# A four-layer attention and expert kernel: depooled rows by index gather, keys moved to layer 2, the last expert pair inside layer 3, select masks, turned maxima

## The chip, the cores and the metric

The kernel runs on one core of one Trainium2 chip. Its time is the device time of one execution in microseconds (us); the median of several runs is given. The profile comes from one more execution with the hardware profiler on. The engines are called PE (TensorE matmul), PEld (TensorE weight load), DVE (VectorE), ACT (ScalarE), POOL (GpSimd) and SP (SyncE, which here issues most of the DMAs).

## The reference

The input `x` is 16 batches of 256 tokens of 256 numbers. It passes through four layers, each an attention followed by a feed-forward part. `ctx` is 16 x 256 x 512.

- Layer 0: layer norm, causal-length masked self-attention with 16 heads of 16 and a bias; then 8 experts (256 to 1024 to 256, gelu), top 2, each expert with a capacity.
- Layer 1: the "depool". From the patches of `ctx` a decayed scan over the 256 patch positions of a batch gives `depool`; for each token an index `plug` picks one of its rows. The core of it:

```python
_, s = jax.lax.associative_scan(comb, (a_b, u), axis=1)
depool = s.reshape(bsz, plen, D_MODEL)
plug = jnp.clip(jnp.cumsum(boundary_mask, axis=1) - 1, 0, plen - 1)
depool_out = depool[jnp.arange(bsz)[:, None], plug]
return depool_out + h
```

  with `h` the doubly normalised token times `W_in`. Then a feed-forward part with 8 routed experts (top 2) and a shared one.
- Layer 2: a cross-attention with 8 heads of 32 over keys and values from `ctx`, then causal self-attention with 16 heads of 16, then 4 unlike experts (2 chosen of 4).
- Layer 3: a cross-attention with 8 heads of 32 over keys and values from `ctx`, and a linear layer with fake fp8 quantisation, whose scale needs the maximum over all batches.

Softmax is taken with the true row maximum subtracted. All matmuls are float32 (two passes on PE each, as the records of the profile count them) except masks and selections, which are bfloat16.

## The kernel before

All of it is one program, in the order of the layers. Each stage is a loop over batches, or over experts. The activations `xs[b]` stay on chip as tiles of 128 x 2 x 256 (two halves t of 128 tokens). Where many batches overlap, the order of the instructions is written by hand: `order` is a pair of lists, one for even and one for odd steps s, of entries (function, lag, arguments). In step s each entry runs its function for batch s - lag (`do`, L432, skips batches outside 0 to 15). Inside `manual_schedule` the engines get their instructions exactly in this order, so every engine works through a queue of its own and waits for what is missing.

Stretches in time (us from the start of the span), with lines:

- **0 to 355, layer 0** (L536 to L760): attention with `heads_transposed` (L277: four 128x128 transposes into one PSUM tile, then an evacuation by ACT), `maxima` (L631), `exps`, `values`. Softmax subtracts the row maxima by an extra row of the head's padding: `maxima` (DVE, L635) writes minus the maximum into column 17 of the padded queries `qpads`; then `queries(..., QMs)` transposes those padded queries a second time, maximum included, so `QM` times `kpad` gives scores less maxima. `score_max` and `probs` (L223, L241) each take four PSUM banks of the pool `pmm` (six banks in layer 0 and layer 3, four in layer 2). Routing, and `scatter` (L730), which zeroes and fills the experts' buffers in DRAM.
- **355 to 410**: constants of layer 1, and keys and values of the first `KV0 = 3` batches for layers 2 and 3 (`kv_load`, `kv_piece`, L476 to L516: four pieces a batch of eight passes each).
- **410 to 882, layer-0 experts** (L889 to L928): 8 experts, weights by DMA, `pmm` and `pacc` matmuls of 512 and 256 columns. In between, DVE computes the patch ends and the plug indices (`mark`, `plugs`, L837 to L850); for batches 0 and 1 `patch_load`, `patch_norm` and `patch_scan` (L854 to L885) run here.
- **882 to 1118, depool** (L930 to L1040): `gather` (four indirect DMAs a batch on POOL, L945), `summed` (L951: adds the experts' rows, layer norm moments, a second norm by `rms_of_normed`, seven small POOL operations), `norm1`, `turned1`, `depool` (L976), `norm2`, `experts_in`, `gates`; and, for batches 2 to 15, `patch_load`, `patch_norm`, `patch_scan`; and `kv_bring`/`kv_part` for batches 3 to 15. The row `plug` is picked by a matmul: `patch_scan` transposes the plug column (L882), compares it with the partition number (L885) into a one-hot `take`, and `depool` multiplies `take` with `dep` (L984) in the same PSUM group as `W_in` (L982).
- **1118 to 1553**: router and shared expert, then 36 expert blocks of layer 1.
- **1553 to 2643, layer 2** (L1276 to L1812): one order for the cross-attention (class `Heads32`, L297), the self-attention, and the expert work of earlier batches. The experts work on pairs of batches: `f_in`, `f_turned`, `f_part`, `f_end` (L1659 to L1747) with lags 3 to 5. The steps start some 57 to 60 us apart; the first four hold no expert work, and after 2490 only expert work of the last pair is left. Causal masks are strips of bfloat16 matmuls into PSUM: `mask` before the maxima, `maskT` before the exps (both `strips`, L1471; the matmul is L1475). Weights come by `fetch` (L1639). Reciprocal square roots are two POOL operations (`rsqrt`, L154 to L158).
- **2643 to 2711, overflow** (L1815 to L1871): experts whose token count exceeds half of their region do the rest in blocks under `tc.If`, with all experts' weights loaded once beforehand (`FW`); sizes 128, 128, 256, 512, 512, 512. In this input expert 0 has 318 tokens past the half, expert 1 none, expert 2 30, expert 3 124.
- **2711 to 3010, layer 3** (L1880 to L2045): weights and constants, the first batches' loads, norms and queries, then the attention, order L2033 to L2045 (`fetch`, L1969, is an indirect DMA on POOL).
- **3010 to 3068**: maximum over all `zn`, and the fp8 linear layer.

Of the kernel before, what the change touches and what calls it, by code (L numbers as in the profile page):

```python
# [31 lines left out]
KV0 = 3  # L32

# [5 lines left out]
def tile_kernel(ctx: ExitStack, tc: tile.TileContext, a, out):  # L39
# [39 lines left out]
    selw = ct([P, 2, P], "selw")  # L79
    V.memset(selw, 0.0)  # L80
    for c in range(2):
        for j in range(4):
            for k in range(3):
                G.affine_select(
                    selw[:, c, :], selw[:, c, :], [[0, P]], ALU.not_equal, 1.0,
                    base=-(32 * j + 2 * k + c), channel_multiplier=1,
                )
    V.tensor_copy(sel, selw)
# [80 lines left out]
    def ln_stats(b, premul=1.0):  # L169
# [6 lines left out]
        r = small(2, "lnr")  # L176
# [9 lines left out]
    def rms_of_normed(mv, r, eps):  # L186


        q = small(2, "rmsq")
        G.tensor_tensor(q, r, r, ALU.mult)  # L190
        G.tensor_tensor(q, q, mv[:, :, 1], ALU.mult)
        rr = small(2, "rmsr")
        rsqrt(rr, q, 1.0, eps, 2)
        return rr
# [45 lines left out]

    def probs(cp, kc, QT, KT, n, bias, scale, minus=None, mask=None, causal=False):  # L241

        q0 = kc * P if causal else 0
        sc = [pmm().rearrange("p (i q) -> p i q", i=2)[:, :, q0:] for j in range(4)]
        if mask is not None:
            for j in range(4):
                mask(sc[j], j)
        for i in range(2):
# [5 lines left out]
            for j in range(4):  # L254
                rows = slice(32 * j, 32 * j + n)
                T.matmul(  # L256
                    sc[j][:, i, :], lhsT=KT[rows, c, kc * P : (kc + 1) * P], rhs=QT[rows, c, q0:],
                    start=(minus is None and mask is None), stop=True, skip_group_check=(mask is not None),
                )
# [17 lines left out]
    def heads_transposed(dst, src, h0, on=None, scale=None):  # L277
# [4 lines left out]
        evac(dst, p, scale, on=on)  # L282

# [160 lines left out]
    with ExitStack() as l01:  # L444
# [26 lines left out]
        b_key = col(a["b_src"][:D], 2, "b_key", c01)  # L471
        b_val = row_bc(a["b_src"][D:], D, "b_val", c01)
        mcol = t01([P, NT], "mcol")
# [58 lines left out]
        with ExitStack() as l0:  # L532
# [6 lines left out]
            bk = c0.tile([B, S], F32, name="bk")  # L539
# [22 lines left out]

            kpads, vpads = [], []
            for i in range(3):
                k = c0.tile([P, 4, S], F32, name=f"kpad{i}")
                V.memset(k, 1.0)
# [18 lines left out]
            def load(b):  # L585
# [17 lines left out]
                dma(ye2[n0 : n0 + 512, :].rearrange("(p r) d -> p (r d)", p=P), zero[:, : 4 * (D - 64)])  # L603
                if b == B - 1:
# [13 lines left out]
            def q_norm(b):  # L618
                mv, r = mvs.pop(b)
                qps[b] = qpads[2 * (b % 2) : 2 * (b % 2) + 2]  # L620
                for t in range(2):
                    normed(qps[b][t][:, :, :16], b, t, mv, r, split=16)
                    G.memset(qps[b][t][:, :, 17], 0.0)
# [4 lines left out]
            def queries(b, t, to):  # L628
                heads_transposed(to[b][:, :, t * P : (t + 1) * P], qps[b][t], 0, A)
# [1497 lines left out]
```

## Time and profile before

| | us |
|---|---|
| median of 3 runs | 3068.09 (3065.16 to 3077.72) |
| the profiled execution's own time | 3069.45 |
| its span in the trace | 3067.6 |
| mean granted clock of TensorE | 0.949 |

So 1.85 us of the profiled execution lie around the span. A page of the profile is read like this: first the busy time of each engine; then the span in 40 slices of 76.7 us; then DMA queues; then the chain of work that ended last; then groups of instructions by line, with mean duration in ns, and the idle time in front of them and what ended it. "PEclk" is the TensorE clock that the throttle granted, as a part of full speed.

Busy time by stage, from the same trace:

| stretch | length | PE | DVE | ACT | POOL | PEclk |
|---|---|---|---|---|---|---|
| 355 to 410, transition | 55 | 33.39 | 20.30 | 4.77 | 38.81 | 0.73 |
| 1118 to 1265, router, shared expert | 147 | 139.51 | 45.79 | 17.04 | 61.69 | 0.97 |
| 1265 to 1553, expert blocks | 288 | 286.18 | 66.02 | 53.55 | 9.86 | 1.00 |
| 3010 to 3068, fp8 linear | 58 | 24.55 | 42.22 | 21.33 | 24.39 | 0.55 |

A busy share is a mean over the stretch; a PE at 1.00 of its clock and near the whole stretch busy has no room, one at 0.57 with half of the time idle has.

### The profile page before, as it was taken

Reading aid. Unit: us, or ns where it says so; the run is one execution under the profiler, and the core shown is the slowest. Engines: PE = TensorE matmul, PEld = TensorE weight load, DVE = VectorE, ACT = ScalarE, POOL = GpSimd, SP = SyncE. Lnnn points to the kernel's source line nnn. Section 1 sums busy time; section 2 is a strip of 40 time slices with the busy share of each in tenths; the row PEclk is TensorE's granted clock in tenths of the full one; section 3 lists DMA queues with packets and bytes.
Section 4 is the critical chain, followed back from the end, with each engine's and each line's share of the span. In section 5 each row is a group of like instructions: output and inputs, shape, how many; then the busy total and the mean of one; then the engine's idle time right before and its main releaser. Section 6 shows DMA issues by size and latency. Waiting matters only on the chain. (4 is left out here: it accounts for less than half of the span.)

```text
span 3067.6 us, 57308 instructions
## 1 busy us (share of the span) xinstructions
PE 2807.7 (92%) x22567; PEld 2021.2 (66%) x22567; DVE 1475.1 (48%) x3848; ACT 1160.2 (38%) x2192; POOL 912.5 (30%) x1459
## 2 busy tenths in 40 slices
PE   7999799999989999999958789999999999759995
PEld 4666566666668865788834457777777777646663
DVE  7777611100027653222235666666666551038876
ACT  3555421121112221111113446566666664225453
POOL 2356620000036516200021333323333221045633
PEclk9999899999999999999967999999999999869996
DMA  6851232122135523666530113343333236342211
GB/s 251 343 194 57 74 109 85 56 69 78 40 101 180 161 90 126 222 198 200 183 120 18 34 55 102 103 128 107 102 120 99 90 98 208 97 136 64 67 35 55
DMA packets 249375, 357.07 MB, mean 116 GB/s; under 512 B 24107, under 2 KB 189019, under 8 KB 244868
## 3 DMA queue, kind: packets, MB, share of 16 engines
q1 hardware_dynamic: 230660, 305.75, 30.7%
q0 software_dynamic: 18432, 47.47, 4.8%
q8 instruction: 187, 3.06, 0.4%
q14 instruction: 96, 0.79, 0.1%
HBM read 236.40 MB, written 117.52 MB: 115 GB/s over the span
## 5 line engine op out<-in xcount | busy, mean ns | idle before, releaser
L263 ACT ACTIVATE big<-pmm 128x512 f32<-128x512 f32 (+1 forms) x512 | 237.0, 549 | 105.9 <-PE pmm L256 105.7
L909 PE MATMUL pmm<-xiT,w 128*128 128x512 f32 x512 | 225.3, 598 | 2.0 <-DVE xiT L145 2.0
L157 POOL TENSOR_SCALAR rsq<-mv 128x2 f32<-128x2 f32 x128 | 26.3, 206 | 666.8 <-DVE mv L175 652.1
L917 PE MATMUL pacc<-w,h 128*128 128x256 f32 x1024 | 223.6, 379 | 0.0
L918 DVE COPY yo<-pacc 128x256 f32<-128x256 f32 x64 | 27.2, 424 | 403.5 <-PE pacc L917 403.5
L917 PEld LDWEIGHTS pacc<-w,h 128*128 128x128 f32 x1024 | 194.6, 190 | 33.3 <-issue 7.7
L945 POOL DMA_INDIRECT y<-ye,idx x64 | 62.3, 974 | 481.5 <-issue 481.1
L635 DVE TENSOR_REDUCE qpad<-pmm 128x2 f32<-128x512 f32 x256 | 158.8, 684 | 55.0 <-PE pmm L234 54.4
L909 PEld LDWEIGHTS pmm<-xiT,w 128*128 128x128 f32 x512 | 96.1, 191 | 120.9 <-issue 111.8
L316 DVE TENSOR_REDUCE max<-pmm 128x2 f32<-128x512 f32 x256 | 158.4, 680 | 26.6 <-PE pmm L234 26.3
L1492 DVE TENSOR_REDUCE qpad<-pmm 128x2 f32<-128x256 f32 (+1 forms) x256 | 124.9, 551 | 70.0 <-PE pmm L234 70.0
L1676 PE MATMUL pf<-hf,fw 128*128 128x256 f32 x640 | 152.5, 381 | 0.0
L1376 POOL DMA_INDIRECT y<-yslots,idx x64 | 66.1, 1033 | 284.1 <-SPq L1259 267.9
L1676 PE MATMUL pf<-xf,fw 128*128 128x256 f32 x576 | 142.7, 384 | 0.1
L911 ACT ACTIVATE h<-pmm 128x512 f32<-128x512 f32 x128 | 76.4, 597 | 150.8 <-PE pmm L909 150.8
L1676 PEld LDWEIGHTS pf<-hf,fw 128*128 128x128 f32 x640 | 116.8, 190 | 15.6 <-issue 2.0
L272 PE MATMUL pacc<-big,vpad 128*32 128x256 f32 (+1 forms) x2048 | 121.2, 360 | 0.1
L1676 PEld LDWEIGHTS pf<-xf,fw 128*128 128x128 f32 x576 | 103.2, 190 | 18.6 <-issue 6.7
L174 DVE BATCH_NORM_STATS2 bnst<-x 128x6 f32<-128x256 f32 x256 | 104.3, 407 | 4.8 <-POOL x L656 2.0
L234 PE MATMUL pmm<-kpad,QT 32*128 32x256 f32 x1024 | 103.4, 415 | 2.2 <-DVE qpad L635 1.0
L281 PE MATMUL ptr<-ident,qpad 128*128 128x128 f32 x512 | 85.0, 290 | 21.2 <-DVE qpad L184 12.4
L234 PE MATMUL pmm<-KT,QT 32*128 32x256 f32 (+1 forms) x1536 | 98.0, 369 | 1.4 <-DVE QT L2008 1.4
(462 smaller groups left out, 6091.6 us busy)
## 6 DMA issues: line engine op xcount, KB each, us to landing
xe<-zero SPq DMA_DIRECT2D x24, 1024.0 KB
w<-in_w_dram SPq DMA_DIRECT2D x16, 1024.0 KB
wg<-in_w_gate_dram SPq DMA_DIRECT2D x36, 352.0 KB
wu<-in_w_up_dram SPq DMA_DIRECT2D x36, 352.0 KB
xslots<-zero SPq DMA_DIRECT2D x9, 1024.0 KB
wd<-in_w_down_dram SPq DMA_DIRECT2D x36, 256.0 KB
xi<-xslots SPq DMA_DIRECT2D x36, 256.0 KB
yslots<-yb SPq DMA_DIRECT2D x36, 256.0 KB
```

The source lines that it names most:

```text
L174: V.bn_stats(st, xs[b][:, t, :])
L234: T.matmul(sc[j][:, i, :nk], lhsT=QT[rows, c, t * P : (t + 1) * P], rhs=KT[rows, c, :nk], start=(mask is None), stop=True, skip_group_chec ...
L263: A.activation(e[:, :, q0:], sc[j], AF.Exp, bias=bias, scale=scale)
L272: T.matmul(O[32 * j : 32 * j + 32, i, q0:], lhsT=lhsT(kc, 8 * cp + 4 * i + j), rhs=pT[j][:, i, q0:], start=(kc == 0 and i == 0), stop=(kc ...
L281: T.transpose(p[:, c, :], src[:, h0 + 4 * c : h0 + 4 * c + 4, :].rearrange("p h d -> p (h d)"), ident)
L316: V.tensor_reduce(self.m[:, t, j, :], sc, AX.X, ALU.max, negate=True)
L635: V.tensor_reduce(qps[b][t][:, 8 * cp + j : 8 * cp + j + 5 : 4, 17], sc, AX.X, ALU.max, negate=True)
L909: T.matmul(p, lhsT=w1[:, c, f * P : (f + 1) * P], rhs=xiT[:, c, :], start=(c == 0), stop=(c == 1))
L911: A.activation(h, p, AF.Gelu_apprx_tanh)
L917: T.matmul(p[:, :D], lhsT=hT[f][:, s * P : (s + 1) * P], rhs=w2[:, f, :], start=(f == 0), stop=(f == 7))
L1492: V.tensor_reduce(qp[:, 8 * cp + j : 8 * cp + j + 5 : 4, 16], sc, AX.X, ALU.max, negate=True)
L1676: T.matmul(p[:, j * S : (j + 1) * S], lhsT=w[:, c, f * P : (f + 1) * P], rhs=x, start=(c == 0), stop=(c == len(src) - 1),)
```

## The change

Seven edits go together.

1. **Depooled rows by gather.** `patch_scan` writes its result to DRAM (`depd[b]`), a new `patch_rows` gathers the rows by two indirect DMAs with `plug` as index and writes them to `takd[b]`, `taken_rows` brings them back in the depool stage, and `depool` adds them by a DVE operation in SBUF. One-hot, its transposes and its matmuls go. All 16 batches' `patch_load`, `patch_norm`, `patch_scan` stand in the layer-0 experts.
2. **Keys and values.** Batches 3 to 8 (`KV1 = 9`) stay in the depool stage, 9 to 15 are computed in layer 2's first steps, in buffers of the experts' pool.
3. **Last pair and overflow.** The expert pair of batches 14 and 15 leaves layer 2's loop and is interleaved with layer 3's first two steps; the overflow then runs between layer 3's step 1 and step 2, with its weights loaded inside the If, in sizes 128, 256, 512, 512, 512, 128. Layer 3 has four `pmm` banks and a pool of two (`pf2`) for queries and the final product.
4. **Select masks.** The exps of layer 2 run unmasked, and POOL sets the masked part of each result to 0 by `affine_select`; `maskT` goes.
5. **Turned maxima.** Layers 0 and 2 transpose the maxima alone (one 128x128) and add them to the transposed queries on DVE, in place of four transposes and an evacuation by ACT.
6. **Norms.** `ln_twice` computes the twofold norm from one reciprocal root (two POOL operations for seven); in the depool stage the normalisations go from DVE to ACT (`to_norm`).
7. **Orders.** New lists for layer 0 (scatter lag up to 29), depool, layer 2 (x_load lag -11) and layer 3; four more transfers of zeroes into `ye2`; a ring of 15 for 12.

```diff
-        r = small(2, "lnr")
-    def rms_of_normed(mv, r, eps):
-        q = small(2, "rmsq")
-        G.tensor_tensor(q, r, r, ALU.mult)
-        G.tensor_tensor(q, q, mv[:, :, 1], ALU.mult)
-        rr = small(2, "rmsr")
-        rsqrt(rr, q, 1.0, eps, 2)
-        return rr
+    def ln_twice(b, eps):
+        mv, s2 = ln_moments(b), small(2, "s2")
+        rsqrt(s2, mv[:, :, 1], 1.0 + eps, 1e-5 * eps, 2)
+        return mv, s2
...
+    def less_maxima(QM, QT, t, mx):
+        p, tok = ptr()[:, :P], slice(t * P, (t + 1) * P)
+        T.transpose(p, mx.rearrange("p j c -> p (j c)"), ident)
+        V.tensor_tensor(QM[:, :, tok], QT[:, :, tok], p.unsqueeze(1).to_broadcast([P, 4, P]), ALU.add)
...
             def queries(b, t, to):
-                heads_transposed(to[b][:, :, t * P : (t + 1) * P], qps[b][t], 0, A)
+                if to is QMs:
+                    less_maxima(QMs[b], QTs[b], t, mx0[b % 2][t])
+                else:
+                    heads_transposed(to[b][:, :, t * P : (t + 1) * P], qps[b][t], 0, A)
...
         def patch_scan(b):
-            p = ptr()
-            for lc in range(2):
-                T.transpose(p[:, lc * P : (lc + 1) * P], plug[:, lc, b : b + 1].to_broadcast([P, P]), ident)
-            take = takes[b] = wp.tile([P, 2, S], F32, name="take", tag="take", bufs=4)
-            for c in range(2):
-                V.tensor_scalar(take[:, c, :], p[:, :S], iop[:, c : c + 1], None, ALU.is_equal)
+            dma(depd[b].rearrange("(c p) d -> p c d", p=P), dep)
+
+        def patch_rows(b):
+            y = wp.tile([P, 2, D], F32, name="rows", tag="rows")
+            for t in range(2):
+                G.indirect_dma_start(
+                    out=y[:, t, :], out_offset=None, in_=depd[b],
+                    in_offset=bass.IndirectOffsetOnAxis(ap=plug_rows[:, t, b : b + 1], axis=0),
+                )
+            dma(takd[b], y)
...
-                if e > 5:
-                    patch_load(e - 6)
-                    patch_norm(e - 6)
-                    patch_scan(e - 6)
+                for b in (2 * e, 2 * e + 1):
+                    patch_load(b)
+                    patch_norm(b)
+                    patch_scan(b)
+                for b in range(6 * e - 30, min(6 * e - 24, B)):
+                    if b >= 0:
+                        patch_rows(b)
...
             def depool(b):
-                        T.matmul(p[:, t, :], lhsT=hT[:, c, tok], rhs=w_in[:, c, :], start=(c == 0), stop=False)
-                    for c in range(2):
-                        T.matmul(p[:, t, :], lhsT=take[:, c, tok], rhs=dep[:, c, :], start=False, stop=(c == 1))
+                        T.matmul(p[:, t, :], lhsT=hT[:, c, tok], rhs=w_in[:, c, :], start=(c == 0), stop=(c == 1))
                 V.tensor_tensor(xs[b], xs[b], p, ALU.add)
+                V.tensor_tensor(xs[b], xs[b], deps.pop(b), ALU.add)
...
             def exps(b, u):
-                pTs[b, u] = probs(u // 2, u % 2, QMs[b], KTs[b], 32, 0.0, 1.0, None, maskT, True)
+                kc = u % 2
+                pTs[b, u] = probs(u // 2, kc, QMs[b], KTs[b], 32, 0.0, 1.0, causal=True)
+                for e in pTs[b, u]:
+                    e = e[:, :, kc * P : (kc + 1) * P]
+                    G.affine_select(e, e, [[0, 2], [1, P]], ALU.is_ge, 0.0, base=0, channel_multiplier=-1)
...
+            tail = [B - 2]
             def f_part(b, odd, u, j):
-                if b % 2 == odd:
+                if b % 2 == odd and b < tail[0]:
...
+                def more(e, FW, many, n0, sizes):
+                    if sizes:
+                        with tc.If(many > n0):
+                            if not FW:
+                                FW = [weight(fx, n, k * P, n0, n1, tag=f"w{i}") for i, (n, k, n0, n1) in enumerate(names[e])]
+                            tokens(e, FW, n0, sizes[0])
+                            more(e, FW, many, n0 + sizes[0], sizes[1:])
...
-            psums(l3a, "ps4", 6, 1, 1)
+                psums(l3a, "ps4", 4, 1, 1)
...
-            for s in range(-13, B + 2):
+                with tc.manual_schedule(engines=BUSY):
+                    for s in range(-44, 2):
+                        for f, lag, *more in order[s % 2]:
+                            do(f, s - lag, *more)
+                l2f.close()
+                past_regions()
...
+                with tc.manual_schedule(engines=BUSY):
+                    for s in range(2, B + 3):
+                        for f, lag, *more in order[s % 2]:
+                            do(f, s - lag, *more)
```

The layer-3 order after the change also holds entries `(late, lag, f, ...)`, which run one piece of the last expert pair in the step equal to their lag, from -44 to 1. The new layer-2 order holds `(kv_one, lag, j, i)`: in the step equal to its lag it runs piece i of batch j's keys and values (i = 4 is the load).

## The prediction

> **What bounds the kernel now.** I read the page's busy shares first, then the table of stages (busy time of each engine in stretches that I cut at stage borders), then the waits and groups of the stages that the change touches, and last the timeline where a price was needed.
>
> ```profile
> PE 2807.7 (92%) x22567; PEld 2021.2 (66%) x22567; DVE 1475.1 (48%) x3848; ACT 1160.2 (38%) x2192; POOL 912.5 (30%) x1459
> ```
>
> TensorE is the bound, but 92% is a mean over unlike stages. The stages, in order of time (stretch, its length, then PE, PEld, DVE, ACT, POOL busy with counts, granted clock, DMA share, GB/s):
>
> ```profile
> 0.00:355.00 355.00, 326.99 (x3635) 210.44 (x3635) 266.91 (x649) 194.94 (x371) 170.78 (x280) 1.00 0.53 193
> 410.00:882.00 472.00, 467.68 (x1747) 311.89 (x1748) 50.95 (x135) 91.10 (x157) 2.87 (x5) 0.99 0.21 65
> 882.00:1118.00 236.00, 209.25 (x1045) 183.00 (x1043) 150.97 (x408) 54.99 (x131) 133.00 (x235) 0.92 0.50 160
> 1553.00:1615.00 62.00, 30.17 (x212) 16.25 (x213) 25.06 (x53) 8.40 (x14) 21.37 (x31) 0.57 0.42 131
> 1615.00:1843.00 228.00, 187.41 (x2132) 110.20 (x2132) 137.32 (x374) 89.59 (x187) 64.83 (x113) 0.88 0.11 35
> 1843.00:2490.00 647.00, 646.77 (x7389) 484.61 (x7388) 408.15 (x1182) 406.51 (x753) 208.44 (x365) 1.00 0.34 106
> 2490.00:2643.00 153.00, 147.13 (x1120) 122.79 (x1119) 34.88 (x123) 66.58 (x126) 22.15 (x37) 1.00 0.54 173
> 2643.00:2711.00 68.00, 41.29 (x212) 36.87 (x212) 3.87 (x10) 15.79 (x40) 0.00 (x0) 0.72 0.08 23
> 2711.00:2740.00 29.00, 7.44 (x26) 4.54 (x30) 10.33 (x34) 3.68 (x5) 17.48 (x27) 0.57 0.71 230
> 2740.00:3010.00 270.00, 259.90 (x2956) 172.19 (x2948) 212.32 (x486) 131.88 (x235) 136.85 (x187) 0.98 0.21 60
> ```
>
> PE is full in the layer-0 experts (410 to 882) and in eleven steps of layer 2 (1843 to 2490): there only removed PE work counts, and added work costs its whole length. Layer 1's depool (882 to 1118) has PE idle for 27 us and POOL as the next engine. From 2490 to 3010 PE idles 65 of 520 us, most of it in the overflow blocks (27) and the prelude of layer 3 (22).
>
> **Layer 0 (0 to 355), term -8.** The prices are from layer 2's timeline, where PE has no gaps:
>
> ```profile
> 2101.53 0.33 PE L1475 MATMUL pmm<-tri,ident_bf 32*32 32x256 bf16 x16
> 2101.79 0.73 PE L234 MATMUL pmm<-KT,QT 32*128 32x128 f32 x16
> 2102.45 0.66 PE L281 MATMUL ptr<-ident,kpad 128*128 128x128 f32 x4
> 2103.02 1.24 PE L1525 MATMUL pmm<-woT,aoT 128*128 128x192 f32 x6
> ```
>
> From start to start, four transposes take 0.57 us and sixteen mask strips 0.26 us. For each of 32 half batches three of four transposes go: 0.43 x 32 = 13.8 us of PE. ACT's evacuation (0.69 us) becomes a DVE add of 512 columns; L985, an add of that shape, takes 0.68 us, so DVE gains 22 us on top of 267 of 355. DVE's maxima release PE's banks, so the ends are -14 (all beside PE) and -14 + 22 = +8; I take -8. The transition to 410 (three kv batches, POOL-bound tables) stays: 0.
>
> **Layer-0 experts, term +20.** Fourteen patch scans come here. One is six passes of 256 columns at 0.216 us (four passes span 0.86 us in dense stretches): 1.3 us, 14 x 1.3 = 18 in a stage with 4 us of idle PE. Loads, norms and the row gathers fall to queues that are idle here (POOL 2.9, DVE 51 of 472). With a little for the scan's wait on its norm: +20, ends +14 and +26. The depooled rows' way through DRAM (a write, two gathers, a write, a read a batch) I cost at nothing: DMA is busy 21% here, and the rows are read at the earliest 100 us later; uncovered, a read would cost about what the block loads of the overflow cost below, 4.7 us. The same holds for layer 0's four more zeroing writes.
>
> **Layer 1's depool, term -60.** PE loses seven kv batches (6.9 us each from start to start, 48), the products with the one-hot (128 passes, 27.6), its 30 transposes (4.3) and 87 passes of scans (18.8): 209 becomes 110. POOL is then level:
>
> ```profile
> L945 POOL DMA_INDIRECT y<-ye,idx x63 | 61.3, 972 | 45.2 <-issue 44.7
> L158 POOL TENSOR_TENSOR lnr<-rsq,neghalf 128x2 f32<-128x2 f32 x32 | 24.0, 750 | 2.7
> L158 POOL TENSOR_TENSOR rmsr<-rsq,neghalf 128x2 f32<-128x2 f32 x16 | 11.1, 696 | 1.3
> ```
>
> and among the stage's waits (in total, times, longest):
>
> ```profile
> POOL rsq L157 <- DVE mv L175: 46.1, 19, 10.0
> ```
>
> POOL's 133 plus 17 of issue between gathers, less the second norm's five operations a batch (27) and the scans' own rsqrt (13), leaves 110, or 6.9 us a batch; it also waits 46.1 us (2.9 a batch) for DVE's moments. DVE loses the one-hots and the normalisations (23, which go to ACT) and gains an add of 0.68 a batch: below 100. Today the first depool stands 27 us behind the start, the last 17 ahead of the end, with 12.9 us a batch between. I take 6.9 plus two thirds of that wait, 8.8: 27 + 15 x 8.8 + 17 = 176, so -60. Ends: POOL without gaps (6.9: -89), and today's pace if gather, norm and product turn into one chain (0).
>
> A rule that speaks against the added adds: the Trainium skill, "SBUF — State Buffer", § Who interferes with whom, says that a DVE instruction with two SBUF inputs and a GpSimd instruction that reads SBUF lock each other out for the whole instruction. This trace shows no such lengthening: the same kind of DVE operation runs beside a POOL busy 56% of the time, and its 64 instances keep within 14 ns.
>
> ```profile
> L953 DVE SCALAR_TENSOR_TENSOR x<-y,wk,x x64: 473/484/487, 859.5 to 1080.1; 128x256 f32<-128x256 f32 x64
> ```
>
> By the rule, if each of the 16 new adds waited for one POOL operation of 0.75 us, 12 us would come on top (an estimate); I take 0.
>
> **Router, shared expert, expert blocks (1118 to 1553):** untouched, 0.
>
> **Layer 2, term -10.** Four exps a batch lose 0.26 us of strips each (1.04), and the turned maxima save 2 x 0.43 = 0.86: 1.9 us a batch, x 11 dense steps = -21. In the first four steps PE is not the bound (187 of 228), nor in the lead-in (30 of 62). Into those 73 us of idle PE go seven kv batches, 48 us. The pieces stand at fixed places of an order in which the attention chain sets the pace, so I let a quarter stick out: +11. Ends: -30 (all 16 batches save, kv hidden), +27 (kv uncovered, -21 kept). POOL gets 16 selects a batch: the nearest row, L806, an affine_select of 128x256, takes 0.389 us, 6.3 a batch on top of 19 in a step of 59, and is cover only while POOL isn't late.
>
> **From 2490 to 3010, term -12.** The last FFN pair now runs beside layer 3's preparation and first two steps: its 6 us of idle and the prelude's 29 us go, -35. Expert 0's overflow of 318 tokens takes blocks of 128 and 256 in place of 128, 128 and 256: one block less, 8 us by its start-to-start on the timeline. But each expert's weights are now loaded inside its If, where they were loaded ahead. Row for a load that nothing hides:
>
> ```profile
> PE ptr L1824 <- DMA xi<-xe: 23.6, 5, 9.9
> ```
>
> 4.7 us a block, at most 9.9: for three experts +13 (ends 0 and +30). Layer 3 stops and refills around the overflow: +5 (0 to +12), by the clock of 0.57 and 7.4 us of PE work in today's prelude. The rule "TensorE: Matmul & The Clock Gate", § What's actually happening, of the Trainium skill has the clock halve after an idle window of about 3.4 us and come back after as long a busy one. It agrees with the 0.57 and 0.72 above in kind, and would price four gaps at 4 x 1.7 = 7 us (an estimate).
>
> Layer 3's scores keep 4 banks instead of 6. A group of four takes PE 1.4 us and DVE or ACT 2.45 us, about 3.9 in sum; four groups a batch make 15.7 of today's 16.5, so 0.8 us of slack. DVE's reciprocal (1.74 us, L380) stands between two reduce groups, and could put 1 us a batch on the path for 13 batches: +13 (0 to +30). Sum -35 - 8 + 13 + 5 + 13 = -12; ends -43 and +37.
>
> **Sum.** -8 + 20 - 60 - 10 - 12 = -70, off the profiled execution's 3069.45 us (span 3067.6), which lies 1.4 above the median of 3068.09: **3000**.
>
> **Rivals.**
> Forecast, 2965 to 3040: chance 0.50.
> (1) Depool runs at POOL's floor and layer 3 pays nothing for 4 banks and weights: -8 + 20 - 89 - 10 - 38 = -125, 2945 (2925 to 2965). For it: POOL has 46 us of waits to give. Against it: gathers land late already (DVE waits 20.2 us for them). Chance 0.17. Further down: 0.04.
> (2) The change takes work off PE in depool, but gather, moments, rsqrt, norm and product of one batch then follow each other at the old 12.9 us: -70 + 60 = -10, 3059 (3040 to 3080). For it: seven kv batches that filled PE's waits are gone. Chance 0.17.
> (3) Slower: a select in layer 2 stands on POOL, which works in order, behind an rsqrt that waits for DVE, and values wait for the select:
>
> ```profile
> POOL rsq L157 <- DVE mv L175: 280.1, 21, 19.8
> ```
>
> That is 13.3 us a wait. If one group of selects a batch is caught, and 5 us of other PE work stand between exps and values, PE loses 8.3 x 16 = 133: 3000 + 133 = 3133. It makes the kernel slower than before from 70 / 16 = 4.4 us a batch. Against it: the new orders issue statistics after the exps that are read next. Chance 0.12.
>
> **How the numbers follow.** The likeliest gives 3000. The range takes in the forecast, rivals 1 and most of 2: 2925 to 3075. About what a measurement can tell from no change is 0.5%, 15 us: from 2 some 0.07 falls below 3053 and 0.10 between 3053 and 3083. Faster 0.50 + 0.17 + 0.04 + 0.07 = 0.78, same 0.10, slower 0.12.
>
> **What will show it.** The depool stage 176 us with POOL above 60% busy; layer-0 experts 492; eleven layer-2 steps of 57 us with PE full and no PE wait on a select; no stretch like 2711 to 2740, but one PE gap of about 40 us inside layer 3; layer-3 batches near 17.5 us. I am wrong if depool keeps 12 us a batch, if values wait for POOL, or if the break in layer 3 costs over 70 us.

## The result and the profile after

The changed kernel takes 3090.92 us (median of 4 runs, 3090.39 to 3094.01) against 3068.06 for the kernel before: a ratio of 1.0071, 95% interval 1.0048 to 1.0094. It is slower by 0.7%, where 3000 us were forecast, 2.2% faster than before. The profiled execution took 3090.39 us with a span of 3088.7.

The page of the changed kernel, first line:

```profile
PE 2779.6 (90%) x21165; PEld 1987.4 (64%) x21165; DVE 1503.3 (49%) x3878; ACT 1153.6 (37%) x2189; POOL 1010.3 (33%) x1542
```

PE is busy for 28 us less, and the span grew by 21, so PE stands idle for 49 us more than before. Where, the table of stages of the changed kernel shows (columns as in the prediction; the borders are moved to the same instructions):

```profile
0.00:361.00 361.00, 326.53 (x3545) 206.28 (x3545) 284.95 (x686) 179.67 (x340) 170.34 (x252) 1.00 0.54 192
416.00:907.00 491.00, 483.13 (x1821) 324.93 (x1822) 69.03 (x175) 105.84 (x209) 42.31 (x61) 1.00 0.30 99
907.00:1076.00 169.00, 124.74 (x587) 105.80 (x585) 102.11 (x302) 64.45 (x129) 98.59 (x131) 0.82 0.54 166
1513.00:1579.00 66.00, 38.94 (x260) 24.54 (x261) 27.33 (x62) 9.31 (x16) 19.13 (x25) 0.70 0.55 170
1579.00:1849.00 270.00, 229.06 (x2065) 149.54 (x2065) 155.69 (x410) 89.95 (x192) 85.22 (x152) 0.86 0.17 54
1849.00:2499.00 650.00, 640.33 (x6613) 478.91 (x6612) 430.28 (x1192) 392.71 (x731) 276.16 (x482) 1.00 0.34 105
2499.00:2688.00 189.00, 166.02 (x1194) 134.61 (x1196) 60.85 (x194) 77.02 (x143) 64.34 (x106) 0.95 0.50 158
2688.00:2780.00 92.00, 43.44 (x279) 34.77 (x272) 10.81 (x24) 17.65 (x39) 1.21 (x2) 0.73 0.25 78
2780.00:3030.00 250.00, 243.14 (x2718) 159.83 (x2717) 188.43 (x436) 121.39 (x217) 122.41 (x168) 0.99 0.18 49
```

The exact account goes by the starts of instructions that both kernels have:

| from, to | before | after | difference | forecast |
|---|---|---|---|---|
| span's start, first product of the layer-0 experts | 412.1 | 418.1 | +6.0 | -8 |
| to their last product | 468.7 | 488.2 | +19.5 | +20 |
| to the first product of the shared expert (depool) | 237.7 | 170.2 | -67.5 | -60 |
| to layer 2's first projection | 496.1 | 502.2 | +6.1 | 0 |
| to layer 2's last projection | 879.1 | 923.8 | +44.7 | -10 |
| to layer 3's last product | 516.0 | 527.3 | +11.3 | -12 |
| to the span's end | 57.9 | 58.9 | +1.0 | 0 |

The layer-0 experts and the depool stage come out near their terms; layer 0 does not. The largest loss is in layer 2, and there in two parts: its first four steps, without expert work (called the ramp below), take 269.9 us instead of 228.5 (+41.4), and the eleven steps after them (the dense steps) take 59.1 us each where they took 58.8 (+3.3), though nearly 2 us of PE work a step are gone. Steps are counted from the first projection (L1470) of one batch to that of the next. Of the +6.1 before layer 2's first projection, 5.0 lie behind the first expert block, where the first pieces of the keys and values now run as well (kv_in_d, without them, has +2.9 there).

**The ramp of layer 2.** PE's timeline of the changed kernel in one ramp step:

```profile
1680.11 3.72 PE L519 MATMUL pmm<-wsrc,kvx 128*128 128x256 f32 x16 [0.76 <-DVE mx L1526]
1683.76 0.32 PE L1515 MATMUL pmm<-tri,ident_bf 32*32 32x256 bf16 x12
1684.61 0.29 PE L1515 MATMUL pmm<-tri,ident_bf 32*32 32x256 bf16 x4 [0.54 <-DVE big L522]
```

The piece of the keys and values (L519) first waits for a score bank that the maxima on DVE still hold. Then the fourth bank of the next scores waits for the DVE addition that empties the piece (L522). The piece does not slip into a gap: it stands in the queue of the same four banks and gives DVE work that the chain waits for. PE's idle time in the ramp is 41 us, as it was before (269.9 less 229.0 busy, 228.5 less 187.9).

**The dense steps.** Two places where PE waits in a step of the changed kernel, in time:

```profile
2097.33 0.63 PE L280 MATMUL ptr<-ident,qpad 128*128 128x128 f32 x4 [0.65 <-DVE qpad L1493]
...
2130.82 0.73 PE L255 MATMUL pmm<-QM,KT 32*128 32x128 f32 x16
...
2133.34 1.95 PE L255 MATMUL pmm<-QM,KT 32*128 32x256 f32 x16 [0.29 <-ACT big L262]
```

A group of 16 score products at 256 columns takes 1.15 us where nothing holds it (at 2092.66). Here it takes 1.95, and the wait in front of it ends with ACT's exps, which empty the banks of the group 2.5 us ahead; that its inner delay has the same cause is read from this, not shown. From start to start, over the eleven steps, strips and query transposes fell by 19 us (the new transposes of the maxima counted), and the products of the exps (+10), the key transposes (+5) and small rises elsewhere took that back.

POOL is not what PE's products wait for; only its weight loads wait for a select, 13 times and 2.4 us in all. In the dense steps of the changed kernel POOL's waits are led by the selects themselves, which wait for ACT:

```profile
POOL big L1535 <- ACT big L262: 234.2, 44, 16.6
```

**The last pair and the break.** Waits between the last projection and the overflow, changed kernel (in total, times, longest):

```profile
POOL y L2042 <- DMA ye<-yo: 51.2, 2, 48.8
DVE x L2051 <- DMA y<-ye,idx: 42.9, 2, 39.6
...
PE pf L1714 <- DVE hf L1732: 16.1, 1, 16.1
```

Read from the bottom: PE waits 16 us for an activation of the last pair that DVE finishes. DVE works in order, and ahead of it stands layer 3's addition of gathered rows, which waits 39.6 us. Its gather on POOL waits 48.8 us until expert rows are written, the last of them by the same pair (issued at 2634.3 us, the gather starts at 2639.1). Layer 3's first steps were to fill the pair's tail; in a common queue they stop it.

In the break itself (2696 to 2777, the last product before the overflow to the first behind it) the blocks wait for their rows, whose loads stand behind the weights' loads in the code:

```profile
PE ptr L1897 <- DMA xi<-xe: 39.5, 4, 18.6
```

Four blocks wait 39.5 us, where five waited 23.6 before; the two longest, 18.6 and 10.8 us, are where a new expert's weights come in.

### The profile page after: what moved, and what is told of

Its sections match the earlier page's. It is cut to its first block, busy times and chain, and to the rows that moved or that the text cites. A ratio compares the mean times of both kernels' runs of the same rounds, so it can differ in the third digit from the quotient of the medians.

```text
span 3088.7 us, 54737 instructions
## 1 busy us (share of the span) xinstructions
PE 2779.6 (90%) x21165; PEld 1987.4 (64%) x21165; DVE 1503.3 (49%) x3878; ACT 1153.6 (37%) x2189; POOL 1010.3 (33%) x1542
## 5 line engine op out<-in xcount | busy, mean ns | idle before, releaser
L262 ACT ACTIVATE big<-pmm 128x512 f32<-128x512 f32 (+1 forms) x512 | 236.8, 549 | 112.2 <-PE pmm L255 111.3
L1535 POOL TENSOR_SCALAR_AFFINE_SELECT big<-big 128x256 f32<-128x256 f32 x256 | 108.4, 440 | 395.3 <-ACT big L262 387.6
L659 DVE TENSOR_REDUCE mx<-pmm 128x2 f32<-128x512 f32 x256 | 158.9, 684 | 27.3 <-PE pmm L236 26.8
L1526 DVE TENSOR_REDUCE mx<-pmm 128x2 f32<-128x256 f32 (+1 forms) x256 | 124.9, 550 | 68.8 <-PE pmm L236 68.8
L159 POOL TENSOR_SCALAR rsq<-ss 128x2 f32<-128x2 f32 x32 | 6.1, 192 | 377.2 <-ACT junk L887 261.0
L271 PE MATMUL pacc<-big,vpad 128*32 128x256 f32 (+1 forms) x2048 | 127.4, 368 | 0.1
L159 POOL TENSOR_SCALAR rsq<-mv 128x2 f32<-128x2 f32 x144 | 29.5, 205 | 298.7 <-DVE mv L177 262.2
L2042 POOL DMA_INDIRECT y<-ye,idx x64 | 63.7, 995 | 157.1 <-SPq L1939 90.0
```

What stands on the lines that cost most here:

```text
L262: A.activation(e[:, :, q0:], sc[j], AF.Exp, bias=bias, scale=scale)
L271: T.matmul(O[32 * j : 32 * j + 32, i, q0:], lhsT=lhsT(kc, 8 * cp + 4 * i + j), rhs=pT[j][:, i, q0:], start=(kc == 0 and i == 0), stop=(kc ...
L659: V.tensor_reduce(mx0[b % 2][t][:, j, 17 + 2 * cp : 19 + 2 * cp], sc, AX.X, ALU.max, negate=True)
L1526: V.tensor_reduce(mx[:, j, 16 + 2 * cp : 18 + 2 * cp], sc, AX.X, ALU.max, negate=True)
L1535: G.affine_select(e, e, [[0, 2], [1, P]], ALU.is_ge, 0.0, base=0, channel_multiplier=-1)
```

## The experiments

The runs came in three sets, each on a chip of its own. On the chips of the second and third the kernel before takes 3187.83 and 3189.34 us, and the changed kernel 3215.78 (third). Times of these two sets are compared only with each other, or by ratios to the kernel before on the same chip; the times in the expectations are those of the first result and the first set. The two chips agree where the same code ran on both: layer 2 of the changed kernel has dense steps of 61.0 us on both (old_order0, after_again) and a ramp of 274.0 and 276.7.

**Undo one edit each (first set; the kernel before 3071.35 us there).**

*kv_in_d*: `kv_one` out of layer 2, all 13 batches at the old lags in the depool stage.

```diff
-                (kv_one, 4, 6, 4), (experts_in, 5), (kv_one, 0, 4, 0), (kv_one, 12, 8, 0), (kv_one, 6, 6, 1),
+                (kv_part, -5, 2), (experts_in, 5), (kv_part, -2, 0), (taken_rows, -3), (kv_part, -5, 3), (gates, 7),
...
+            order = [[x for x in o if x[0] is not kv_one] for o in order]
             for s in range(-11, B + 5):
```

> The changed kernel with edit 2 undone: all 13 batches' keys and values in the depool stage at the old lags, none in layer 2. In the changed kernel layer 2's first four steps take 67.5 us each (57.1 before), 270 in all against 228.5, and PE is idle for 41 us of them as before. Theory 'no cover': the seven moved batches (48 us of PE) cost nearly their whole length there, because PE's gaps are short waits inside the attention chain, and the pieces take score banks and add DVE and ACT work to that chain. Then the four steps go back to 57 us (-41). The depool stage has 44 us of idle PE in 169, so it grows by less than 48, to 185 to 205. Total 3066 to 3086. Rival 'the new order': the steps are longer because of the new order of layer 2 itself; then they stay above 64 us and the total rises to 3100 or more.

Measured: 3096.22 us, ratio 1.0088 (1.0066 to 1.0109). The depool stage takes 194.8 us, +24.6. The four ramp steps take 249.0, -20.9. Neither theory is right alone: half of the ramp's growth is the keys' (21 of 48 us stick out, not 11), and 20 us stay without them. The ramp without the keys:

```profile
1601.40:1850.40 249.00, 202.09 (x1888) 121.67 (x1889) 147.53 (x395) 84.43 (x180) 84.68 (x151) 0.77 0.11 33
```

PE idles for 47 us of it, 6 more than before, and is busy for 14 us more with 244 products fewer: the granted clock is 0.77 here, 0.88 in the kernel before and 0.86 with the keys in. So most of the 20 us are the same products at a lower clock, and most of the keys' cover is not idle time either: with them in, PE idles 6 us less, and its other products take some 18 us less. What lowers the clock was not tried.

The move as a whole is worth about nothing: 25 us gained in the depool stage, 21 to 23 paid in layer 2. In the depool stage with all the keys PE has 162.55 us of work in 194.8, so there they found cover for half of their length, too:

```profile
907.40:1102.20 194.80, 162.55 (x815) 141.46 (x813) 113.86 (x326) 70.42 (x143) 94.70 (x131) 0.91 0.60 189
```

*strips_back*: mask strips on PE, no selects.

```diff
-                pTs[b, u] = probs(u // 2, kc, QMs[b], KTs[b], 32, 0.0, 1.0, causal=True)
-                for e in pTs[b, u]:
-                    e = e[:, :, kc * P : (kc + 1) * P]
-                    G.affine_select(e, e, [[0, 2], [1, P]], ALU.is_ge, 0.0, base=0, channel_multiplier=-1)
+                pTs[b, u] = probs(u // 2, u % 2, QMs[b], KTs[b], 32, 0.0, 1.0, None, maskT, True)
```

> The changed kernel with edit 4 undone: bfloat16 mask strips on PE before layer 2's exps, no selects on POOL. In the dense steps PE's own time for strips and transposes fell by 19 us, and PE's time at the exps' score matmuls, at the key transposes and elsewhere rose by as much. Theory 'the bank is late anyway': PE stood in the strips while ACT was still emptying the banks, so the strips cost almost nothing: 3086 to 3095, dense steps within 0.3 us of 59.2. Theory 'select': the selects hold the values matmuls back and that is what ate the gain; then strips back and selects out gives dense steps of 58.5 or less and 3080 or less. Theory 'strips are real': 16 x 1.04 = 17 us slower, 3108.

Measured: 3087.12 us, ratio 1.0059 (1.0037 to 1.0080), not apart from the changed kernel. Dense steps 59.7 (+0.6), ramp 262.5 (-7.4, where another run with the same layer 2, tail_back, has 265.9). So strips cost PE 0.6 of the 1.04 us a step that they were priced at. What the selects cost in the ramp stays open, as two runs with the same ramp lie 4 us apart. The theory "select" falls: no product waits for one. But the selects are not free either. With the strips back, the exps' products take 40.2 us over the eleven steps for 48.2, and the key transposes 12.2 for 16.7 (38.1 and 11.7 in the kernel before): two thirds of what the strips cost is had back there. The key transposes wait for DVE's padded keys and queries (L1493), and those take up to 623 and 627 ns where selects run beside them, with medians of 418 and 424 where not (last section).

*turned_back2*: transposes and evacuation back in layer 2.

```diff
-                if to is QMs:
-                    less_maxima(QMs[b], QTs[b], t, mx2[b % 2][t])
-                else:
-                    heads_transposed(to[b][:, :, t * P : (t + 1) * P], qpads[t], 0, A, hw[:, 0:1])
+                heads_transposed(to[b][:, :, t * P : (t + 1) * P], qpads[t], 0, A, hw[:, 0:1])
```

> The changed kernel with edit 5 undone in layer 2 only: the padded queries are transposed again with the maxima in them, ACT evacuates them, no add on DVE. Theory 'late anyway': transposes of 0.35 us net, twice a batch, are given back by less waiting: 3086 to 3095. Theory 'DVE': the two adds of 0.69 us a batch sit on DVE ahead of what PE waits for (key and query rows, L280 waits); then it is faster, 3075 to 3086. If the transposes are real PE time: 16 x 0.7 = 11 slower, 3102.

Measured: 3112.48 us, ratio 1.0144 (1.0121 to 1.0167). Dense steps 60.5, +1.4, well above the 0.86 they were priced at. All three expectations are missed to the same side; the edit saves 1.4 us a step in this order. Undone one at a time, then, edits 4 and 5 save 2.0 us a dense step, and the step is no shorter than before. Something else in layer 2 had to cost that.

*tail_back*: pair, overflow and layer 3 as before.

```diff
-            tail = [B - 2]
+            tail = [B]
...
-        tail[0] = B
+        l2f.close()
+        with ExitStack() as l2e:
```

> The changed kernel with edit 3 undone: the last expert pair in layer 2's loop, then the overflow with all weights loaded ahead, then layer 3 with six score banks and the old order. In the changed kernel the stretch from the last projection to the last product of layer 3 takes 527 us against 516 before: PE waits 19 us in the pair for products that stand on DVE behind the adds of layer 3's gathered rows, whose gathers wait for the expert rows to be written; and the break for the overflow takes 81 us. Theory 'the break': undoing it gives back 10 to 20 us, 3071 to 3081, with a pair tail of about 150, an overflow of 68, a prelude of 29 and 270 of layer 3. Rival: the loss comes in with the last steps of layer 2's new order (the pair has lost its place there), and stays: 3086 to 3095.

Measured: 3077.68 us, ratio 1.0023 (1.0011 to 1.0036): 13 us off the changed kernel, and the stretch to layer 3's last product goes from 527.3 to 513.9 us. The theory "the break" holds as far as its time goes: edit 3 costs 13 us. The run undoes the pair's move, the break and the four banks together, so the shares of the three are read from the trace alone.

**Old orders with the new operations (second set; the kernel before 3187.83).**

*old_order2*: kv_in_d with the kernel before's `order` for layer 2. *old2_tail*: the same with tail_back.

```diff
-                (kv_one, 4, 15, 0), (f_part, 5, 1, 7, 0), (f_part, 5, 1, 7, 1), (kv_one, 4, 15, 1), (kv_one, -8, 9, 4),
+                (maxima, 1, 2), (heads_q, 1, 0, QMs), (f_part, 5, 1, 7, 1), (normed_again, 1), (f_part, 5, 1, 8, 0),
```

> As the run kv_in_d (no keys and values in layer 2), but layer 2 in the kernel before's hand-written order, with the selects and the turned maxima kept. So far: with kv gone the first four steps still take 62.2 us (57.1 before); strips back made dense steps 0.6 us longer and turned maxima undone 1.4 longer, so those two edits save 2.0 us a dense step, yet the dense step is no shorter than before (59.2 against 59.1). Theory 'the order': the new order itself costs about 2 us a dense step and 5 a step in the ramp; with the old one dense steps take 57.0 to 57.6 and the first four 57 to 59: 20 + 20 us off kv_in_d, 3050 to 3060. Rival 'the banks': the scores' four banks set the dense step at 59 whatever PE saves; then only the ramp shrinks, 3073 to 3082.

> As old_order2, with edit 3 undone too (pair 14/15 in layer 2's loop, overflow and layer 3 as before). tail_back alone took 13 us off the changed kernel. If the break's price does not depend on layer 2's order, this stands 10 to 16 us below old_order2: 3035 to 3050, faster than both kernels. If the old order pushes the pair's work into a longer tail of its own, as it was before, the gain is under 5.

Measured: old_order2 3257.50 us, ratio 1.0205 (1.0171 to 1.0238), dense steps 63.7, ramp 258.6; old2_tail 3254.88 us, 1.0200 (1.0168 to 1.0233), its end 9 us shorter, of which the total shows 2.6, within the noise: the 13 us of tail_back do not show here. The dense steps of old_order2, with 43 us of idle PE where the changed kernel has 10 (22 in after_again):

```profile
1943.70:2644.10 700.40, 657.43 (x6617) 478.34 (x6616) 432.82 (x1203) 395.04 (x731) 278.03 (x489) 0.99 0.31 98
```

The theory that the new order is simply the worse one falls, and so does the rival: with the new operations the old order is worse still.

*old_order0*: only layer 0's lists put back. *old_all*: old2_tail with them.

```diff
-                (exps, -1, 0), (scatter, 29, 2), (back, 0, 0), (maxima, -2, 1), (q_norm, -3), (values, -1, 0),
+                (maxima, -2, 1), (back, 0, 1), (scatter, 16, 1), (exps, -1, 1), (values, -1, 0), (q_norm, -3),
```

> The changed kernel with only layer 0's order lists (and their scatter lags) put back. Layer 0 now has a period of 19.45 us a batch (20.4 before) but starts its second half of the pipeline 8 us later. Theory 'turned maxima give the period': the old order keeps about 19.5 and fills sooner: layer-0 experts start at 410 to 415 (418 to 420 now), total 3082 to 3090. Rival 'the new order gives it': with the old order the adds on DVE are waited for, the period is 20.4 or more and the experts start at 425 or later: 3097 or more.

> old2_tail with layer 0's old order as well: what is left of the change is the gather, the scans in the experts, selects, turned maxima and ln_twice. By the sums of the theories, old2_tail plus the difference of old_order0: 3030 to 3050. By the rivals (banks, new order gives layer 0's period) 3070 to 3085.

Measured: old_order0 3229.92 us, 1.0117 (1.0083 to 1.0150), experts from 460.4; old_all 3265.06 us, 1.0230 (1.0197 to 1.0264), experts from 462.6, against 446.2 in old2_tail. "The new order gives it" holds: with the turned maxima, the old order makes layer 0 14 to 16 us longer than the new one.

**The pairs completed (third set; the kernel before 3189.34).**

*order2_alone*: new order of layer 2 with the old operations (kv_in_d, strips_back and turned_back2 at once). *turned_back0*: old operation in layer 0, new order. *gather_only*: everything undone but edits 1 and 6, with the depool stage's new order, the new buffer pools and the four transfers of zeroes kept. *after_again*: the changed kernel.

```diff
             def queries(b, t, to):
-                if to is QMs:
-                    less_maxima(QMs[b], QTs[b], t, mx0[b % 2][t])
-                else:
-                    heads_transposed(to[b][:, :, t * P : (t + 1) * P], qps[b][t], 0, A)
+                heads_transposed(to[b][:, :, t * P : (t + 1) * P], qps[b][t], 0, A)
```

> The changed kernel with the keys back in the depool stage and both layer-2 edits (selects, turned maxima) undone: layer 2 has the old operations in the new order. Theory 'the order was made for the new operations': dense steps 61 to 61.5 us (59.1 before with the old order, 59.2 in the changed kernel), since strips back cost 0.6 and transposes back 1.4 a step; ramp 235 to 245. Total 20 to 30 us above the changed kernel. Rival 'only the operations matter': dense steps 59 to 59.5, ramp 228 to 232: 10 to 20 us below it. What the ramp has over 228.5 here is the order's, what it has less than 249 is the operations'.

> The changed kernel with edit 5 undone in layer 0 only, new order kept. By the term of the prediction, transposes at 0.43 us each of 32 times: period 19.45 + 0.86 = 20.3, the experts start 8 to 14 us later than in the changed kernel, of which the simpler filling of layer 0 gives 2 back. If the DVE adds take the gain, the start is within 3 us.

> What is left of the change is edit 1 and edit 6: gathered depool rows, all scans in the layer-0 experts, one reciprocal root for the twofold norms. Keys and values in the depool stage, layer 0, layer 2 and layer 3 as before. From the runs so far: depool with 13 batches of keys 195 us against 236 before (-41), the experts +19.5, the rest as before: 21 us faster than the kernel before, ratio 0.992 to 0.995. Rival: if ln_twice or the other pools slow layer 0 or layer 2 (four zeroing writes more, a longer ring), 0.997 to 1.002.

> The changed kernel itself, as the reference on this chip for the three others: 1.0071 (1.0048 to 1.0094) of the kernel before, as measured first.

Measured: order2_alone 3234.38 us, 1.0139 (1.0105 to 1.0173); turned_back0 3216.80, 1.0077 (1.0048 to 1.0106); gather_only **3167.34, 0.9933 (0.9912 to 0.9954)**; after_again 3215.78, 1.0084 (1.0055 to 1.0113). Layer 2's ramp and dense steps in gather_only (old order, old operations):

```profile
1671.00:1901.00 230.00, 186.57 (x2132) 110.54 (x2132) 137.51 (x374) 89.71 (x188) 63.25 (x102) 0.89 0.12 35
1901.00:2560.00 659.00, 648.99 (x7389) 483.87 (x7388) 407.49 (x1182) 406.38 (x753) 201.75 (x331) 1.00 0.33 104
```

and in order2_alone (new order, old operations):

```profile
1688.00:1939.00 251.00, 200.56 (x2137) 120.23 (x2138) 139.16 (x388) 89.62 (x190) 63.33 (x104) 0.82 0.10 33
1939.00:2625.00 686.00, 663.49 (x7382) 487.29 (x7381) 408.15 (x1169) 404.60 (x754) 202.24 (x328) 1.00 0.31 99
```

The number of products is the same within ten, and between these two kernels nothing in these stretches differs but layer 2's order: with the old operations it makes the ramp 20.3 and the eleven steps 27.6 us longer. Of the 20.3, PE idles 6.9; the rest is the same products at a granted clock of 0.82 for 0.89. On the two slower chips, in one table (old_order2 and old_order0 are of the second set):

| | layer 2: four ramp steps | a dense step | layer-0 experts begin |
|---|---|---|---|
| old order, old operations (gather_only) | 230.3 | 59.9 | 437.3 |
| old order, new operations (old_order2; old_order0) | 258.6 | 63.7 | 460.4 |
| new order, old operations (order2_alone; turned_back0) | 250.6 | 62.4 | 448.5 |
| both new, with keys in the ramp (after_again) | 276.7 | 61.0 | 446.9 |

The theory "the order was made for the new operations" holds for the dense steps: there each half alone is worse than both or none. (Its total of 20 to 30 us above the changed kernel is just missed, by 18.6.) In the ramp the halves do not help each other: with the keys in the depool stage it is 20 us over the old pair's with the new order, whether with the new operations (kv_in_d, 249.0, first set, 228.5 before) or with the old (250.6 against 230.3), and 28 over it with the new operations alone. In layer 0, which takes 25 us more on this chip even where its code is unchanged, the turned maxima gain next to nothing: with the new order the start of the experts is 1.6 us later without them. gather_only came out as expected and is faster than both kernels; its 0.7% is the gathered rows and scans, ln_twice and the depool stage's new order together.

## Why the prediction was wrong

The direction and the time were wrong; 3000 was 91 us too low, and 55 of them are layer 2's (-10 forecast, +44.7 measured). Two slips of arithmetic play no part in the time: the upper end of the last stretch is -35 - 8 + 30 + 12 + 30 = +29 and not +37, and a quarter of 48 is 12, not 11. By its own steps:

- **Layer 1's depool, right.** -67.5 for -60. From the first to the last depool product a batch takes 8.2 us; 8.8 was worked out. POOL is busy 98.59 of 169 us, 58%, where above 60 was expected. The bound was not POOL alone: PE waits 26 us for the normalisations that went to ACT, which wait for DVE, which waits 28 us for POOL's roots. That a pace worked out for POOL came so near is in part luck.
- **Layer-0 experts, right.** +19.5 for +20. With this and the depool stage, edits 1 and 6 with the depool stage's new order are worth 21 us: gather_only shows it whole.
- **Layer 2, failed: "I let a quarter stick out: +11".** The keys' pieces stick out by 21 of 48 us in the ramp, and by 2 more ahead of it (kv_in_d). 73 us of idle PE were taken for room. They were waits inside one chain over four score banks, and the pieces need those banks, and DVE and ACT to empty them: the ramp idles 41 us with the pieces and 47 without. The prediction looked at PE's share and not at what held PE.
- **Layer 2, failed: the order priced at nothing.** The term had no entry for the new order at all. With the old operations it costs 20.3 us in the ramp and 2.5 a dense step (order2_alone against gather_only), 48 us in all. This is no share of the 91 by itself: with the new operations, the new order is 2.7 us a dense step better than the old one (61.0 for 63.7), and order and operations can't be priced apart. What stands in the changed kernel is the pair: +20 in the ramp beside the keys, where nothing was forecast, and the dense steps of the next point.
- **Layer 2, failed: "1.9 us a batch, x 11 = -21".** Measured are +3.3, a miss of 24. Undone one by one, the edits cost 0.6 and 1.4 us a step, 2.0 in sum, close to 1.9, so the size of the operations holds in the new order. But taken work shortens a step only in an order that keeps the engines together: counted from the kernel before, either the new order comes first (+2.5) and both operations give back 1.4, or the operations come first (+3.8) and the order gives back 2.7; on those chips the pair ends 1.1 us longer, on the first one 0.3.
- **From 2490 to 3010, failed: -12 forecast, +11.3 measured; undoing the edit gains 13 (tail_back).** Of the five terms the -35 for hidden idle time failed, by the queues of POOL and DVE shown above. The prelude's 29 us are gone, but between the last projection and the overflow PE idles 23 us (189 less 166) where it idled 6: -29 + 17 = -12 in place of -35, which is the whole miss of this step. The stop for the overflow came out near its terms: 68 - 8 + 13 + 5 = 78 were forecast, 81 measured (so the sign "over 70" could not have told right from wrong). It is no single gap of 40 us: PE idles before four blocks, 18.6 us at the longest. The banks cost less than feared: 16.5 us a batch where 16.3 were needed before, 4 us in all for +13.
- **Layer 0, failed: -8 forecast, +6 measured.** The transposes are saved, but the products of the first exps start 6.0 us later (42.5 for 36.5): 1.7 of it before the first transpose (4.4 us of DVE copies into `kpad` where 2.7 us of memsets stood), the rest in the first batch. The rest is not the copies': in turned_back0, with memsets and the new order, they start at 43.3. From there to the last product of layer 0's values only 1.7 us of the 13.8 come back, and undoing the edit costs 1.6 (turned_back0). That DVE's adds, 18 us more of its time, take the rest is likely and not shown.

Of the rivals, (1) and (2) do not come about. (3) has the right sign and the right layer, and the wrong mechanism: no product's wait is put down to a select, the POOL wait that it priced at 13.3 us is down to 32.3 us in 21 waits, and taking the selects away changes the time by 4 us, not by 133. The account that the runs support, in us: edits 1 and 6 -21, the keys' move -25 in the depool stage and +23 in layer 2, the rest of layer 2 +20 in the ramp and +3 in the dense steps, the pair and the overflow +13, layer 0 +6; together +19 of the 21 by which the span grew. What stays open is which entries of the new layer-2 order cost the 20 us of its ramp, and whether they do so by lowering the clock; only the order as a whole was tried.

## What to carry to other kernels

A stage in which an engine idles is not by itself room for that engine's work: look at what ends each idle stretch, and whether the work put there needs the same buffers and the same other engines. Look at the granted clock beside the busy time as well: here one ramp was 20 us longer with the same products and little more idle time (6 us). In an order written out by hand, price the order by itself: here neither half alone explained the time, and only the two-by-two table did. When a later stage is pulled into an earlier one's tail, check whether any of its first instructions waits for that tail's own result: on an in-order engine that wait stops both.

## What the runs showed of the hardware

- The same program took 4% more on another chip with the same durations of instructions: the changed kernel 3215.78 us against 3090.92, while the 512 exps without a bias (L262) have a mean of 549 ns on both and the selects one of 439 and 440. Between the first product of the shared expert and the first expert block, 137 us became 194, at a granted clock of 0.83 for 0.96. PE's largest wait there ends with nothing that the profile shows (here in old_order0, whose code is the same in this stage), so its cause stays open:

```profile
PE pacc L1126 <- issue: 41.7, 2, 27.8
```

- The rule of the Trainium skill, "SBUF — State Buffer", § Who interferes with whom, by which a DVE instruction with two SBUF inputs contends with a GpSimd instruction that reads SBUF, was weighed against the added DVE additions. Their 16 instances keep between 691 and 694 ns beside a POOL busy 58% of the time, so they show no lengthening. POOL does: of the 32 roots in the depool stage (`rsq` from `mv`, L159) 27 take 187 to 193 ns, and the four that fall into one of these additions 585 to 671. The first line is DVE's, the others are POOL's:

```profile
989.35 0.69 DVE L1024 TENSOR_TENSOR x<-x,taken 128x512 f32<-128x512 f32 x1
988.35 0.19 POOL L159 TENSOR_SCALAR rsq<-mv 128x2 f32<-128x2 f32 x1
989.42 0.67 POOL L159 TENSOR_SCALAR rsq<-mv 128x2 f32<-128x2 f32 x1
```

- In layer 2 the selects and such DVE instructions lengthen each other. Of the 256 selects the 206 that run beside no DVE instruction of the lines L1493 (padded queries and keys) and L1421 (expert rows times weight, added) take 400 to 422 ns; the 50 that do have a median of 585, up to 682. On DVE the padded keys have a median of 418 ns away from the selects and 617 beside them, the expert rows 483 and 619. In strips_back, without selects, the padded keys' median is 418. So the trace agrees with the rule in kind, and here both sides slow down by about 0.2 us an instruction:

```profile
L1535 POOL TENSOR_SCALAR_AFFINE_SELECT big<-big x256: 400/407/682, 1633.2 to 2555.5; 128x256 f32<-128x256 f32 x128
L1493 DVE TENSOR_TENSOR kpad<-qk,rq x32: 411/419/623, 1591.7 to 2510.9; 128x256 f32<-128x256 f32 x32
L1499 DVE TENSOR_TENSOR kpad<-qk,rq x32: 417/418/780, 1589.3 to 2506.6; 128x256 f32<-128x256 f32 x32
```

(The last line is strips_back's; its 780 is one instance.)
